# A diffusion transformer block on one core: maxima transposed in one rounded product and sent in three transfers, with halves of the preparation moved between beats

## The chip, the cores and the metric

The kernel runs on one core of a Trainium2 chip. The core has five engines that run their own instruction streams and meet through semaphores: TensorE (PE in the profile, with its weight loads as PEld), VectorE (DVE), ScalarE (ACT), GpSimd (POOL) and SyncE (SP, which here only issues DMA transfers). The metric is the device time of one execution in microseconds (us); the median of three runs is 724.68 us.

## The reference, cut to what matters

The block works on 16 batches of 256 tokens with 256 channels, 16 heads of 16 channels, and a context of 256 tokens for each batch, all in fp32:

```python
x_norm = modulate(_ln(x), shift_a, scale_a)
q, k, v = split(x_norm @ W_qkv + b_qkv)              # self-attention ("source")
x = x + gate_a * (softmax(q k^T * scale) v @ W_proj + b_proj)
q_c = _ln(x) @ W_qc + b_qc                           # cross-attention ("context")
k_c, v_c = split(_ln(context) @ W_kvc + b_kvc)
x = x + softmax(q_c k_c^T * scale) v_c @ W_cproj + b_cproj
x = x + gate_m * (gelu(modulate(_ln(x), shift_m, scale_m) @ W_mlp1 + b_mlp1) @ W_mlp2 + b_mlp2)
```

A softmax needs the maximum of each row of scores, or any number near it: a shift that is the same for a whole row cancels.

## The kernel before, in words

**Split numbers.** Most products are made from two fp32r halves of each fp32 number, a rounded "high" part (`xTh`, `h_q`) and the remainder, "low" (`xTl`, `l_q`). So each prepared operand takes a pass that writes the high half (by ScalarE) and one that writes the low half (by VectorE as value minus high half, or by ScalarE and GpSimd in two steps: ScalarE copies the full value to a tile `y`, GpSimd subtracts).

**Units.** There are 32 attention units: 16 of sources ("s", self-attention of one batch) and 16 of contexts ("c", cross-attention of one batch). The first five are sources; then s and c alternate, and the last five are contexts. While unit n runs its attention, the kernel prepares units n+1 to n+4 and finishes units n-1 to n-3. In the long middle part there are thus two kinds of unit in turn. In this text an **A unit** is one whose running attention is a context's (n is even): it prepares the queries of a context (`q2`, two units on), transposes the normalized source of unit n+3 (`q3`, kind "s"), and normalizes the context tokens of unit n+4 (`lc`). A **B unit** runs a source's attention: it prepares the queries of a source, transposes the context of unit n+3, and normalizes the source of unit n+4 (`ls`).

**Beats.** A unit has eight beats, `beat(n, k)` for k from 0 to 7, and every engine follows its instructions in program order, SP's transfers included. The order of the work is thus the order of the code in `beat`. In each beat

- PE makes four products `s<-big` (scores of the next unit, one pair of heads, into the PSUM tile `s`) and VectorE takes their maxima, `TENSOR_REDUCE mxs<-s`. The tile `s` has one buffer, so PE's next `s` products wait for the reduction;
- PE makes four products `st<-big` (transposed scores of this unit) and ScalarE takes the exponential (`pt<-st`);
- in beats 1, 3, 5 and 7 PE runs two "lanes": 24 half-height products of two preparations side by side (`ps_q`, `ps_k`, `ps_v`, `ps_P`); in beats 0, 2, 4 and 6 it multiplies probabilities with values (`o<-pt,v`). In beat 1 of every unit, and in beat 5 of B units, eight small transpositions (`psT`) are put between the `s` products of this beat and of the next.

**Maxima.** The scores are shifted by a row that is added to the product: row 63 of each half of the queries' tile holds minus the maximum. Maxima stand with queries on partitions, the row needs them along the free dimension. So in beats 2 and 6 PE multiplies `mxs` with an identity (`o<-ident,mxs`, `m_cols`, L767), just ahead of that beat's `o` products; ScalarE negates the result into a tile `m` (`m_send`, L775), and SP sends it into the rows 63, four transfers each time.

**Divisors.** The sums of the softmax of unit n-1 (`S`) come to VectorE by a transfer (`pull_sums`, issued in beat 0), VectorE takes the reciprocal (`recip`), SP writes it to DRAM (`rd<-S`, `spread`) and reads it back spread over all partitions (`R<-rd`, `back`, L1292); GpSimd multiplies (`U<-U,R`) in beat 0 of the next unit.

**Norms.** For a layernorm VectorE makes statistics of the two halves of the tokens (`BATCH_NORM_STATS2`, `st`) and folds them (`mv`); GpSimd makes the reciprocal root (`rs`, two instructions) and normalizes (`xn`, two instructions). The lines of `beat` that the change touches are L1212 to L1300.

Of the kernel before, what the change touches and what calls it, by code (L numbers as in the profile page):

```python
# [21 lines left out]
def pixart_block(  # L22
# [357 lines left out]
    def transposed(src, name, scale=None, pool=False):  # L380
# [61 lines left out]

        o.full, o.rest_pool, o.place = full, rest_pool, place
# [67 lines left out]
    def to_stack(W, src, bias, dst, which, name):  # L511
# [19 lines left out]
        def high():  # L531
            o.hi = work.tile([P, KC, N], F32R, tag="qkh", name=f"h_{name}", bufs=3)
            for f in range(KC):
                ACT.activation(o.hi[:, f], o.ps[:, f * N:(f + 1) * N], AF.Identity, bias=bias[f])
# [190 lines left out]
    def place_of_max(u, g):  # L725

        w, i = (2 + g // 2, g % 2) if u.n == 0 else (2 + u.n % 2, g - 1) if g in (1, 2) else ((u.n - (g == 0)) % 2, g == 0)
        return mxs[w][:, 8 * i:8 * i + 8].rearrange("p (r a t) -> p r a t", r=2, t=NT)  # L730
# [29 lines left out]
    def m_turn(u, hf, pst=None):  # L760

        if pst is None:
            pst = ps_gen(f"psm_{u.n}_{hf}", SHORT)
        PE.transpose(pst[:16, :P], mxs[2 + hf][:, :16], ident)
        return pst

    def m_cols(w, pst):  # L767

        for j in range(2):
            PE.matmul(pst[32 * j:32 * j + 32, :64], w, ident[:, 64 * j:64 * j + 64], start=True, stop=True,
                      tile_position=(0, 32 * j))

    def m_send(pst, *parts):  # L775


        m = work.tile([64, 64], F32R, tag="m2", name="m2", bufs=1)
        ACT.mul(m, pst[:64, :64], -1.0)
        for u, g, row in parts:  # L780
            for j in range(2):
                to = u.q[63:P:64, 2 * g:2 * g + 2].rearrange("r a (t q) -> r a t q", t=NT)[..., 64 * j:64 * j + 64]
                SP.dma_start(to.bitcast(F32), m[32 * j + row:32 * j + row + 8].bitcast(F32))

    def m_row(u, hf, pst):
# [3 lines left out]
        for g in range(2):  # L789
            a = 4 * hf + 2 * g  # L790
            SP.dma_start(u.q[63:P:64, a:a + 2].bitcast(F32), m[8 * g:8 * g + 8].bitcast(F32))
# [369 lines left out]
    def beat(n, k):  # L1161
# [17 lines left out]
        if k == 4 and q2:  # L1179
            q2.Q.high()  # L1180
            q2.Q.send_high()
# [36 lines left out]
        elif k == 1:  # L1218
# [4 lines left out]
            if lc:  # L1223
                lc.ln[0].steps[0]()
# [5 lines left out]
        elif k == 2:  # L1230
            exps()
            if cur:
                parts = [(cur, 3, 0)] * (n > 0) + [(nxt, 0, 8)] * bool(nxt)
# [4 lines left out]
            if ls:  # L1238
                ls.ln[0].steps[0]()
            elif prev:  # L1240
                p1.recip()
                p1.spread()
            if not (q3 and q3.kind == "c"):
                spare(n)
        elif k == 3:
            if q3:
                q3.T[0].high()
            exps()
            if q3 and q3.kind == "c" and n < nu - 4:
                q3.T[0].full()  # L1250
# [7 lines left out]
            if q3 and q3.kind == "s":  # L1258
                q3.T[0].low()
            if prev and ls:  # L1260
                p1.recip()
                p1.spread()
            if lx and n == nu - 4:
                lx.T[0].parts[2]()
        elif k == 4:
# [5 lines left out]
            if q2:  # L1271
                q2.Q.low()
                q2.Q.send_low()
            if q3 and q3.kind == "c":
                if n < nu - 4:
                    q3.T[0].rest_pool()
                spare(n, not lc)
            if ls:
                ls.ln[0].steps[1]()
                ls.ln[0].steps[2]()  # L1280
                ls.ready = True
        elif k == 5:
# [13 lines left out]
        elif k == 6:  # L1296
# [141 lines left out]
```

## Time and profile before

| what | us |
|---|---|
| three runs: lowest, median, highest | 722.59, 724.68, 724.86 |
| the profiled execution: its own time | 722.92 |
| its span, from the first to the last instruction | 721.1 |
| an A unit in the middle, from one first reduction to the next (189.84 to 205.24) | 15.40 |
| the B unit behind it (205.24 to 221.02) | 15.78 |
| PE busy in the A unit and in the B unit | 15.18, 15.60 |
| VectorE busy in the two | 13.67, 13.16 |
| ScalarE busy in the two | 12.66, 13.28 |
| GpSimd busy in the two | 9.54, 12.31 |

The attention units fill the span from about 32 us to 510 us; what follows is the MLP, which the change does not touch. The profiled execution is 1.8 us longer than its span. The granted TensorE clock is 1.00 in all stretches.

### The profile page before, as it was taken

What the parts mean: (1) busy time and instruction counts of PE and PEld (TensorE: products, weight loads), DVE (VectorE), ACT (ScalarE), POOL (GpSimd) and SP (SyncE); (2) the same over time, 40 slices, a digit from 0 to 9 for tenths busy, and PEclk for the clock granted to TensorE, in tenths of its full rate; (3) what the DMA queues carried; (4) which work ended last, traced back from release to release, by engine and by line L of the source; (5) the groups of instructions that cost most, each with busy time, mean ns of one, the idle gap of its engine ahead of it and who ended that gap; (6) DMA issues with size and microseconds to landing.
All of it is one profiled execution on the core that took longest, in us unless ns stands there. A gap on an engine that the chain in (4) does not pass through costs nothing.

```text
span 721.1 us, 23569 instructions
## 1 busy us (share of the span) xinstructions
PE 704.2 (98%) x9359; PEld 600.5 (83%) x9359; DVE 566.5 (79%) x895; ACT 551.0 (76%) x956; POOL 520.5 (72%) x519
## 2 busy tenths in 40 slices
PE   9999999999999999999999999999999999999997
PEld 8777788788877878787778787877779999999997
DVE  5878888988888888778888888888765777777753
ACT  5677888888888888787888888877867677676661
POOL 7665778886776768676686698987766988676552
PEclk9999999999999999999999999999999999999999
DMA  7465455354545536454545556545332223223122
GB/s 238 166 201 200 151 185 194 134 182 167 176 161 186 177 138 189 160 177 150 184 164 193 172 186 204 166 153 206 102 104 87 89 59 89 69 66 86 48 59 74
DMA packets 82921, 106.22 MB, mean 147 GB/s; under 512 B 18970, under 2 KB 45916, under 8 KB 82812
## 3 DMA queue, kind: packets, MB, share of 16 engines
q1 hardware_dynamic: 81916, 104.37, 44.0%
q8 instruction: 74, 1.21, 0.8%
q10 hardware_dynamic: 896, 0.35, 0.2%
q14 instruction: 35, 0.29, 0.1%
HBM read 35.89 MB, written 8.98 MB: 62 GB/s over the span
## 4 chain that ended last, share of the span: by engine, by line
PE 75%; DVE 13%; DMA 4%; issue 2%; POOL 2%; SPq 2%; ACT 1%; POOLq 0%; ACTq 0%; DVEq 0%
PE s L51 18%; PE st L51 13%; PE ph L51 12%; PE o L51 10%; DVE mxs L51 9%; PE ps_kc L51 3%; PE ps_q L51 3%; PE ps_P_s L51 2%; PE ps_k L51 2%; PE ps_v_c L51 2%; SPq L51 2%; PE ps_qc L51 2%; DMA x<-in_x_dram 2%; PE ps_v_s L51 1%; DMA U_s<-oT 1%
## 5 line engine op out<-in xcount | busy, mean ns | idle before, releaser
L51 DVE TENSOR_REDUCE mxs<-s 128x4 f32<-128x1024 f32 x252 | 307.6, 1221 | 65.3 <-PE s L51 60.0
L51 ACT ACTIVATE pt<-st 128x1024 f32<-128x1024 f32 x256 | 262.6, 1026 | 74.6 <-PE st L51 70.4
L51 PE MATMUL s<-big 63*128 63x256 f32 x1008 | 132.9, 322 | 10.9 <-DVE mxs L51 4.3
L51 PE MATMUL o<-pt,v 128*32 128x256 f32 x2048 | 141.6, 384 | 0.0
L51 PEld LDWEIGHTS s<-big 63*128 63x128 f32 x1008 | 82.4, 185 | 70.4 <-DVE mxs L51 62.3
L51 PE MATMUL st<-big 64*128 64x256 f32 (+1 forms) x1040 | 112.4, 285 | 0.3 <-ACT pt L51 0.2
L51 PE MATMUL ph<-xTh_m,wself 128*128 128x256 f32 x512 | 99.6, 280 | 0.0
L51 POOL TENSOR_TENSOR hl<-hf,hh 128x512 fp32r<-128x512 f32 x60 | 80.2, 1354 | 19.2 <-ACT hh L51 19.2
L51 PEld LDWEIGHTS st<-big 64*128 64x128 f32 (+1 forms) x1040 | 85.7, 186 | 3.0 <-ACT pt L51 1.4
L51 PEld LDWEIGHTS o<-pt,v 128*32 128x32 f32 x2048 | 67.0, 109 | 21.7
L51 PEld LDWEIGHTS ph<-xTh_m,wself 128*128 128x128 f32 x512 | 81.9, 188 | 1.2 <-issue 0.4
L51 PE MATMUL ph<-xTl_m,wself 128*128 128x256 f32 x256 | 70.9, 277 | 0.0
L51 ACT ACTIVATE hf<-ph,bT 128x256 f32<-128x256 f32 x112 | 47.0, 473 | 20.6 <-PE ph L51 20.3
L51 ACT ACTIVATE hh<-ph,bT 128x256 fp32r<-128x256 f32 x112 | 47.0, 473 | 19.3 <-PE st L51 8.3
L51 PEld LDWEIGHTS ph<-xTl_m,wself 128*128 128x128 f32 x256 | 48.1, 188 | 0.0
L51 DVE TENSOR_SCALAR xn_m<-x,mv_m,rs_m 128x256 f32<-128x256 f32 x28 | 33.5, 1236 | 15.0 <-POOL rs_m L51 15.0
L51 PE MATMUL s<-big,hh 128*128 128x256 f32 x256 | 45.2, 277 | 0.0
L51 POOL TENSOR_SCALAR rs_c<-mv_c 128x2 f32<-128x2 f32 x16 | 3.6, 228 | 53.5 <-DVE mv_c L51 53.3
L51 POOL TENSOR_SCALAR xn_q<-x,mv_q,rs_q 128x256 f32<-128x256 f32 x32 | 38.9, 1226 | 1.7
L51 POOL TENSOR_SCALAR xn_c<-c,mv_c,rs_c 128x256 f32<-128x256 f32 x32 | 38.9, 1226 | 1.7
L51 PE MATMUL st<-big,hh 128*128 128x256 f32 x224 | 39.5, 276 | 0.0
L51 PEld LDWEIGHTS s<-big,hh 128*128 128x128 f32 x256 | 38.7, 188 | 0.0
(225 smaller groups left out, 2156.9 us busy)
## 6 DMA issues: line engine op xcount, KB each, us to landing
big<-h_k SPq DMA_DIRECT2D x32, 256.0 KB
big<-h_kc SPq DMA_DIRECT2D x32, 256.0 KB
big<-h_qc SPq DMA_DIRECT2D x32, 256.0 KB
big<-h_q SPq DMA_DIRECT2D x30, 256.0 KB
big<-l_k SPq DMA_DIRECT2D x16, 256.0 KB
g<-gd SPq DMA_DIRECT2D x16, 256.0 KB
U_s<-oT SPq DMA_DIRECT2D x32, 128.0 KB
R_s<-rd_s SPq DMA_DIRECT2D x16, 256.0 KB
```

Of the source, the lines that this page charges most:

```text
L51: i = f(*a, **k)
```

## The change

**Maxima.** `mxs` becomes fp32r (rounded), 16 columns for each of four sets in place of 32, and the identity gets an fp32r copy. `m_cols` makes one product of 128 columns in one strip of the array; before it made two fp32 products of 64 columns in two strips. The reductions write their columns so that four neighbouring pairs of heads can go in one transfer: in beat 2 there are two transfers, in beat 6 one, of 512-byte rows; before there were four and four, of 256-byte rows.

**Halves.** Where the unit three on is a source (`apart`: A units, and the first units), the source's high half is made in two pieces before and after the exponential of beat 3, its low half in beats 3 and 4, one piece each; the queries' high half is made in two pieces around the exponential of beat 4, and is sent behind it; the queries' low half moves from beat 4 to beat 5.

**The contexts' remainder.** Where the unit three on is a context, ScalarE's copy `y_c` and GpSimd's subtraction in beat 4 go, and VectorE subtracts from PSUM in beat 3.

**Norms.** The context's statistics are made in beats 1 and 2 (one half each) and the norm is folded and applied in beat 2, before in beat 1 and beat 5. The source's statistics move from beat 2 to beats 5 and 6, folding and applying from beat 4 to beat 6.

**Divisors.** The reciprocal is taken in beat 2 in all units (before: beat 3 in B units); `back` is issued at the start of beat 4, before at the end of beat 5.

```diff
-    mxs = const.tile([P, 4, 32], F32, name="mxs")
-    POOL.memset(mxs, 0.0)
+    mxs = const.tile([P, 4, 16], F32R, name="mxs")
+    POOL.tensor_copy(mxs, wz[:, :64].rearrange("p (a b) -> p a b", a=4))
...
+    identr = const.tile([P, P], F32R, name="identr")
+    POOL.tensor_copy(identr, ident)
...
+        def high_of(f):
+            if f == 0:
+                o.xT = [work.tile([P, KC, N], F32R, tag=f"xT{c}", name=f"xT{c}_{name}", bufs=4) for c in "hl"]
+            ACT.activation(o.xT[0][:, f], o.ps[:, f * N:(f + 1) * N], AF.Identity, scale=scale[f])
+        def low_of(f):
+            DVE.scalar_tensor_tensor(o.xT[1][:, f], o.ps[:, f * N:(f + 1) * N], scale[f],
+                                     o.xT[0][:, f], ALU.mult, ALU.subtract)
...
-        for j in range(2):
-            PE.matmul(pst[32 * j:32 * j + 32, :64], w, ident[:, 64 * j:64 * j + 64], start=True, stop=True,
-                      tile_position=(0, 32 * j))
+        PE.matmul(pst[:16, :P], w, identr, start=True, stop=True, tile_position=(0, 0))
...
-        m = work.tile([64, 64], F32R, tag="m2", name="m2", bufs=1)
-        ACT.mul(m, pst[:64, :64], -1.0)
-        for u, g, row in parts:
-            for j in range(2):
-                to = u.q[63:P:64, 2 * g:2 * g + 2].rearrange("r a (t q) -> r a t q", t=NT)[..., 64 * j:64 * j + 64]
-                SP.dma_start(to.bitcast(F32), m[32 * j + row:32 * j + row + 8].bitcast(F32))
+        m = work.tile([16, P], F32R, tag="m", name="m", bufs=1)
+        ACT.mul(m, pst[:16, :P], -1.0)
+        for u, a, n, row in parts:
+            SP.dma_start(u.q[63:P:64, a:a + n].bitcast(F32), m[row:row + 4 * n].bitcast(F32))
...
-        if k == 4 and q2:
-            q2.Q.high()
-            q2.Q.send_high()
+        apart = q3 and q3.kind == "s"
+        if k == 4:
+            if prev:
+                p1.back()
+            if q2:
+                q2.Q.high((0,) if apart else (0, 1))
+            if q2 and not apart:
+                q2.Q.send_high()
...
             if lc:
-                lc.ln[0].steps[0]()
+                lc.ln[0].stat(0)
...
-            if ls:
-                ls.ln[0].steps[0]()
-            elif prev:
+            if prev:
                 p1.recip()
                 p1.spread()
+            if lc:
+                lc.ln[0].stat(1)
+                lc.ln[0].steps[1](False)
             if not (q3 and q3.kind == "c"):
                 spare(n)
+            if lc:
+                lc.ln[0].pow()
+                lc.ln[0].steps[2]()
+                lc.ready = True
         elif k == 3:
-            if q3:
+            if apart:
+                q3.T[0].high_of(0)
+            elif q3:
                 q3.T[0].high()
             exps()
-            if q3 and q3.kind == "c" and n < nu - 4:
-                q3.T[0].full()
+            if apart:
+                q3.T[0].high_of(1)
...
-            if q3 and q3.kind == "s":
-                q3.T[0].low()
-            if prev and ls:
-                p1.recip()
-                p1.spread()
-            if lx and n == nu - 4:
+            if apart:
+                q3.T[0].low_of(0)
+            if lx:
                 lx.T[0].parts[2]()
...
-            if q2:
+            if apart:
+                q3.T[0].low_of(1)
+                if q2:
+                    q2.Q.high((1,))
+                    q2.Q.send_high()
+            elif q2:
                 q2.Q.low()
                 q2.Q.send_low()
             if q3 and q3.kind == "c":
-                if n < nu - 4:
-                    q3.T[0].rest_pool()
                 spare(n, not lc)
-            if ls:
-                ls.ln[0].steps[1]()
-                ls.ln[0].steps[2]()
-                ls.ready = True
         elif k == 5:
...
-            if lc:
-                lc.ln[0].steps[1]()
-                lc.ln[0].steps[2]()
-                lc.ready = True
-            if prev:
-                p1.back()
+            if apart and q2:
+                q2.Q.low()
+                q2.Q.send_low()
+            if ls:
+                ls.ln[0].stat(0)
...
-                    m_send(cur.po[:, 1], (nxt, 1, 0), (nxt, 2, 8))
+                    m_send(cur.po[:, 1], (nxt, 2, 4, 0))
...
+            if ls:
+                ls.ln[0].stat(1)
+                ls.ln[0].steps[1]()
+                ls.ln[0].steps[2]()
+                ls.ready = True
```

The instructions below stand around beats 0 to 6 of the A unit that starts at 189.84 us in the profile (n = 10). First VectorE before; a reduction opens each beat's share, and the first row shown is that of beat 0:

```order
L51 TENSOR_REDUCE mxs<-s 128x4
L51 SCALAR_TENSOR_TENSOR l_kc_3727<-ps_kc_3573,bP,h_kc_3701 128x256 x2
L51 TENSOR_REDUCE mxs<-s 128x4
L51 BN_STATS st_c_3776<-c_3616 128x6 x2
L51 TENSOR_REDUCE mxs<-s 128x4
L51 RECIPROCAL S_s_3660<-S_s_3660 128x32
L51 TENSOR_REDUCE mxs<-s 128x4
L51 SCALAR_TENSOR_TENSOR xTl_s_3832<-psT_s_3737,sc_107,xTh_s_3831 128x256 x2
L51 TENSOR_REDUCE mxs<-s 128x4
L51 SCALAR_TENSOR_TENSOR l_qc_3888<-ps_qc_3736,bP,h_qc_3864 128x256 x2
L51 TENSOR_REDUCE mxs<-s 128x4
L51 BN_AGGR mv_c_3930<-st_c_3776 128x2 x2
```

and in the change, from beat 1's statistics on:

```order
L51 BN_STATS st_c_3699<-c_3533 128x6
L51 TENSOR_REDUCE mxs<-s 128x2x2
L51 RECIPROCAL S_s_3573<-S_s_3573 128x32
L51 BN_STATS st_c_3699<-c_3533 128x6
L51 BN_AGGR mv_c_3737<-st_c_3699 128x2 x2
L51 TENSOR_REDUCE mxs<-s 128x2x2
L51 SCALAR_TENSOR_TENSOR xTl_s_3761<-psT_s_3660,sc_109,xTh_s_3760 128x256
L51 TENSOR_REDUCE mxs<-s 128x2x2
L51 SCALAR_TENSOR_TENSOR xTl_s_3761<-psT_s_3660,sc_109,xTh_s_3760 128x256
L51 TENSOR_REDUCE mxs<-s 128x2x2
L51 SCALAR_TENSOR_TENSOR l_qc_3857<-ps_qc_3659,bP,h_qc_3794 128x256 x2
L51 TENSOR_REDUCE mxs<-s 128x4 x2
```

Beat 2 now holds the reciprocal, one half of the statistics and the fold; beats 3 and 4 hold one piece of `xTl_s` each; the low half of the queries stands in beat 5.

SP's transfers in the same unit, from the second half of the sums (beat 0) to the maxima of beat 6, before:

```order
L51 DMA S_s_3660<-oT_3612 64x1x32
L51 DMA big_79<-l_kc_3727 32x4x512
L51 DMA U_s_3659<-oT_3612 64x512
L51 DMA big_80<-m_3808 2x4x64 x2
L51 DMA big_82<-m_3808 2x4x64 x2
L51 DMA rd_s_3815<-S_s_3660 128x32
L51 DMA big_79<-h_qc_3864 32x4x512 x2
L51 DMA big_79<-l_qc_3888 32x4x512
L51 DMA R_s_3939<-rd_s_3815 128x1x512
L51 DMA big_82<-m_3965 2x4x64 x4
```

and in the change:

```order
L51 DMA S_s_3573<-oT_3529 64x1x32
L51 DMA big_81<-l_kc_3650 32x4x512
L51 DMA U_s_3572<-oT_3529 64x512
L51 DMA big_82<-m 2x4x128
L51 DMA big_84<-m 2x4x128
L51 DMA rd_s_3734<-S_s_3573 128x32
L51 DMA R_s_3792<-rd_s_3734 128x1x512
L51 DMA big_81<-h_qc_3794 32x4x512 x2
L51 DMA big_81<-l_qc_3857 32x4x512
L51 DMA big_84<-m 2x8x128
```

Three transfers of maxima stand where eight stood, and the read `R_s` is now ahead of the three transfers of queries. PE's order is the same but for the product of maxima.

GpSimd in the B unit in front of it, from beat 1's norm to the products with `R` of the next unit's beat 0, before:

```order
L51 TENSOR_SCALAR xn_q_3449<-x_3_2521,mv_q_3443,rs_q_3446 128x256 x2
L51 TENSOR_TENSOR xTl_c_3500<-y_c_3504,xTh_c_3499 128x512
L51 TENSOR_TENSOR t_c_3293<-t_c_3293,x_0_1411 128x512
L51 TENSOR_SCALAR rs_s_3567<-mv_s_3564 128x2
L51 TENSOR_TENSOR rs_s_3567<-rs_s_3567,mhalf 128x2
L51 TENSOR_SCALAR xn_s_3570<-x_3366,mv_s_3564,rs_s_3567 128x256 x2
L51 TENSOR_TENSOR U_c_3323<-U_c_3323,R_c_3614 128x512
```

and in the change:

```order
L51 TENSOR_SCALAR xn_q_3381<-x_3_2477,mv_q_3375,rs_q_3378 128x256 x2
L51 TENSOR_TENSOR t_c_3229<-t_c_3229,x_0_1391 128x512
L51 TENSOR_SCALAR rs_s_3581<-mv_s_3578 128x2
L51 TENSOR_TENSOR rs_s_3581<-rs_s_3581,mhalf 128x2
L51 TENSOR_SCALAR xn_s_3584<-x_3298,mv_s_3578,rs_s_3581 128x256 x2
L51 TENSOR_TENSOR U_c_3255<-U_c_3255,R_c_3459 128x512
```

The subtraction `xTl_c` is gone; the norm of the source keeps its place in the row, and waits for a fold that VectorE now makes in beat 6 in place of beat 4.

More of the change, by code (lines that the diff above doesn't have):

```diff
@@ L529, in second, with high @@
             high()
-        def high():
-            o.hi = work.tile([P, KC, N], F32R, tag="qkh", name=f"h_{name}", bufs=3)
-            for f in range(KC):
+        def high(fs=range(KC)):
+            if 0 in fs:
+                o.hi = work.tile([P, KC, N], F32R, tag="qkh", name=f"h_{name}", bufs=3)
+            for f in fs:
                 ACT.activation(o.hi[:, f], o.ps[:, f * N:(f + 1) * N], AF.Identity, bias=bias[f])
@@ L725, in place_of_max @@
     def place_of_max(u, g):
[L729 to L730 removed]
+        if u.n == 0 or g in (1, 2):
+            w, i = (2 + g // 2, g % 2) if u.n == 0 else (2 + u.n % 2, g - 1)
+            return mxs[w].rearrange("p (r a t) -> p r a t", r=2, t=NT)[:, :, 2 * i:2 * i + 2]
+        i = int(g == 0)
+        return mxs[(u.n - i) % 2][:, 8 * i:8 * i + 8].rearrange("p (r a t) -> p r a t", r=2, t=NT)
     def s_tile(u, g, par, t, bank=None, home=sp):
@@ L788, in m_row @@
         ACT.mul(m, pst[:16, :P], -1.0)
-        for g in range(2):
-            a = 4 * hf + 2 * g
-            SP.dma_start(u.q[63:P:64, a:a + 2].bitcast(F32), m[8 * g:8 * g + 8].bitcast(F32))
+        SP.dma_start(u.q[63:P:64, 4 * hf:4 * hf + 4, :].bitcast(F32), m.bitcast(F32))
     def t_part(u, pair, par):
```

5 lines of the change are left out of this document (3 added, 2 removed).

## Prediction

> **What bounds the kernel now.** I read the page first, then the timelines of an A unit for VectorE and PE, then SP's queue, then the waits.
>
> ```profile
> PE 704.2 (98%) x9359; PEld 600.5 (83%) x9359; DVE 566.5 (79%) x895; ACT 551.0 (76%) x956; POOL 520.5 (72%) x519
> ```
>
> PE is hardly ever idle and no other engine is above 79%. But a share does not say which wait ends last in a beat. VectorE (start, length, what, idle time ahead and its releaser), beats 2 to 6 of the A unit:
>
> ```profile
> 193.80 1.23 DVE L51 TENSOR_REDUCE mxs<-s 128x4 f32<-128x1024 f32 x1
> 195.50 0.35 DVE L51 RECIPROCAL S_s<-S_s 128x32 f32<-128x32 f32 x1 [0.47 <-DMA S_s<-oT]
> 195.87 1.23 DVE L51 TENSOR_REDUCE mxs<-s 128x4 f32<-128x1024 f32 x1
> 197.01 0.87 DVE L51 SCALAR_TENSOR_TENSOR xTl_s<-psT_s,sc,xTh_s 128x256 fp32r<-128x256 f32 x2
> 197.79 1.22 DVE L51 TENSOR_REDUCE mxs<-s 128x4 f32<-128x1024 f32 x1
> 198.93 0.87 DVE L51 SCALAR_TENSOR_TENSOR l_qc<-ps_qc,bP,h_qc 128x256 fp32r<-128x256 f32 x2
> 199.71 1.21 DVE L51 TENSOR_REDUCE mxs<-s 128x4 f32<-128x1024 f32 x1
> 200.84 0.24 DVE L51 BATCH_NORM_AGGREGATE mv_c<-st_c 128x2 f32<-128x6 f32 x2
> 201.53 1.23 DVE L51 TENSOR_REDUCE mxs<-s 128x4 f32<-128x1024 f32 x1 [0.45 <-PE s L51]
> ```
>
> and PE over the same time, with the `o` block of beat 0 on top:
>
> ```profile
> 189.96 1.07 PE L51 MATMUL o<-pt,v 128*32 128x256 f32 x16
> ...
> 194.22 0.25 PE L51 MATMUL o<-ident,mxs 128*32 128x64 f32 x2
> ...
> 194.36 1.03 PE L51 MATMUL o<-pt,v 128*32 128x256 f32 x14
> 195.32 0.51 PE L51 MATMUL s<-big 63*128 63x256 f32 x4
> ...
> 197.26 0.40 PE L51 MATMUL s<-big 63*128 63x256 f32 x4
> ...
> 199.06 0.50 PE L51 MATMUL s<-big 63*128 63x256 f32 x4
> ```
>
> The reader is to compare the end of each `s` block with the start of the next reduction. Beat 3: 195.32 + 0.51 = 195.83, reduction at 195.87. There PE sets the pace, 0.04 us ahead, and VectorE's wait costs nothing: the reciprocal that waited 0.47 us is over at 195.85. In beat 6 VectorE waits 0.45 us for PE. Beat 4: 197.66, reduction at 197.79, right behind the two `xTl_s` (197.01 and 0.78 for the pair). So VectorE is 0.09 us too late. Beat 5: 199.56 and 199.71, 0.11 us too late behind `l_qc`; but the reduction after it (201.53) waits for PE all the same, so this one is absorbed. And `s` of beat 5 (199.06) follows the end of beat 4's reduction (199.01), not the end of the values' products. Hence in an ordinary unit only PE's own work and those 0.09 us can be won.
>
> The other thing to win lies in units with longer beats. The first two groups below are from the unit at 252 us (VectorE, then SP), the third is from the beat 2 of the B unit behind it, the last from the table of waits (total us, times, longest):
>
> ```profile
> 256.16 1.22 DVE L51 TENSOR_REDUCE mxs<-s 128x4 f32<-128x1024 f32 x1
> 258.90 0.35 DVE L51 RECIPROCAL S_s<-S_s 128x32 f32<-128x32 f32 x1 [1.52 <-DMA S_s<-oT]
> 259.17 1.16 DVE L51 TENSOR_REDUCE mxs<-s 128x4 f32<-128x1024 f32 x1
> ```
>
> ```profile
> 257.04 0.60 SPq L51 DMA_DIRECT2D S_s<-oT  x1
> ```
>
> ```profile
> 274.22 0.75 DVE L51 BATCH_NORM_STATS2 st_s<-x 128x6 f32<-128x256 f32 x2 [0.57 <-DMA x<-in_x_dram]
> 274.89 1.20 DVE L51 TENSOR_REDUCE mxs<-s 128x4 f32<-128x1024 f32 x1
> ```
>
> ```profile
> DVE S_s L51 <- DMA S_s<-oT: 8.0, 10, 2.0
> ...
> DVE st_s L51 <- DMA x<-in_x_dram: 3.6, 5, 1.6
> ```
>
> Here beat 2 takes 259.17 - 256.16 = 3.01 us in place of 2.07 (193.80 to 195.87): VectorE's queue stands behind a reciprocal whose sums SP issued only at 257.04.
>
> **The change, part by part.** *The product of maxima (PE).* With it an `o` block lasts 194.22 to 195.39, 1.17 us; without, 1.07. So the two fp32 products cost 0.10. What one fp32r product of 128 columns costs no row shows. The nearest fp32r row is this, of the start, a chain of 12 products of 256 columns:
>
> ```profile
> 10.17 1.39 PE ps_k L51 x12
> ```
>
> 0.116 each, so 0.058 for half the columns: 0.042 won. At the pace of the fp32 pair now there (0.10 for 64 columns) 128 columns in one strip take 0.20: 0.10 lost. I take the fp32r pace, because its row has the same number type; the other end is kept. There are 63 such products (two in 31 units, one in the last). Beat 6 of the 11 middle B units may keep nothing (below), leaves 52: -2.2 us; ends -2.6 and +6.3.
>
> *Halves.* Beats 3 and 4 of an A unit each get one piece of 0.39 (half of 0.78) behind the reduction, ending 0.6 us ahead of PE; the 0.09 us of beat 4 goes in 11 units (n = 2 to 22, each second one): -1.0. The low half of the queries moves into beat 5: 1.14 from the reduction's start to the next instruction (195.87 to 197.01) + 0.78 = 1.92, where PE takes 1.82 (199.71 to 201.53). The 0.10 is absorbed too: the reduction of beat 6 ends at 201.53 + 1.23 = 202.76, and the `s` block that waits for it stands behind `o`, which ends at 202.81 and with two first products of lanes still between:
>
> ```profile
> 201.78 1.03 PE L51 MATMUL o<-pt,v 128*32 128x256 f32 x14
> ```
>
> In units 0 and 1 one half of the sources' statistics comes into the same beat 5: + 0.33 (half of 274.22 to 274.89), so 2.25 against 1.82, 0.43 more; I count +0.25 for each after such slack, +0.5.
>
> *Reciprocals and statistics.* SP in the A unit, ahead of, in and behind beat 2:
>
> ```profile
> 193.62 0.59 SPq L51 DMA_DIRECT2D S_s<-oT  x1
> ...
> 195.76 2.29 SPq L51 DMA_DIRECT2D big<-m  x4
> 198.16 0.33 SPq L51 DMA_DIRECT2D rd_s<-S_s  x1
> ...
> 199.85 0.55 SPq L51 DMA_DIRECT2D big<-l_qc  x1
> 200.59 0.68 SPq L51 DMA_DIRECT2D R_s<-rd_s  x1
> 203.23 2.22 SPq L51 DMA_DIRECT2D big<-m  x4
> ...
> 215.92 0.68 SPq L51 DMA_DIRECT2D R_c<-rd_c  x1
> ```
>
> Four maxima transfers hold SP 2.2 us, one a quarter of it: three fewer in beat 6 bring the sums of the next unit's beat 0 forward by up to 1.65 us, here from 193.62 to about 192, as ScalarE allows. That takes away the long waits: of the 8.0 us, seven ordinary ones are 3.3 and cost nothing; of the other 4.7 the three beats lose 0.94 for each 1.52 waited, 3.0 us in all. The source's statistics, now three beats later, no longer wait for `x`: of 3.6 us one wait of 1.6 is in the prologue; the other 2.0, at the same 0.94 in 1.52, are -1.2. Together -4.2. The new load of beat 2, reciprocal 0.27 (258.90 to 259.17), statistics 0.33, fold 0.24 behind 1.14, is 1.98 against PE's 2.03 (193.80 to 195.83), so nothing if the sums are there by 194.94. The context's remainder, 0.68 on VectorE in beat 3, (an estimate: the pair `xTl_s` does the same work in 0.87) stands in the place of a reciprocal: 1.14 + 0.68 = 1.82, as long as PE's own beat with lanes. GpSimd and ScalarE lose a pass each per B unit: in the rows above nothing waits for either in beats 3 and 4, zero.
>
> *The norm of the source, two beats later.* GpSimd now, the reduction of beat 6, and PE's first transposition of the norm:
>
> ```profile
> 215.73 0.23 POOL L51 TENSOR_SCALAR rs_s<-mv_s 128x2 f32<-128x2 f32 x1
> ...
> 216.86 2.44 POOL L51 TENSOR_SCALAR xn_s<-x,mv_s,rs_s 128x256 f32<-128x256 f32 x2
> 220.65 1.29 POOL L51 TENSOR_TENSOR U_c<-U_c,R_c 128x512 f32<-128x512 f32 x1 [1.36 <-DMA big<-l_q]
> ```
>
> ```profile
> 217.09 1.23 DVE L51 TENSOR_REDUCE mxs<-s 128x4 f32<-128x1024 f32 x1 [0.60 <-PE s L51]
> ```
>
> ```profile
> 222.53 0.22 PE L51 MATMUL psT_s<-ident,xn_s 64*128 64x64 f32 x1
> ```
>
> The fold will end at 217.09 + 1.14 + 0.33 + 0.24 = 218.80; GpSimd takes 215.73 to 219.30, 3.57 us, so 222.37 and two handoffs. PE asks at 222.53. The cover is just used up: zero, but what beat 6's product wins is lost again (why 52, above). `U_c` then moves from 220.65 to about 222.5; three passes of 1.3 us at most end by 226.4, and PE needs them in beat 3, which reduces at 195.87 + 31.18 (both units of the table) = 227.05.
>
> *Transfers moved.* `R` goes ahead of the queries on SP, and waits there for `rd` to land; `l_qc` is issued at about 201.7 (VectorE ends it at 199.71 + 1.14 + 0.87 - 0.09) in place of 199.85, and PE's `s` of the next unit needs it at 204.80 (0.44 ahead of the reduction of 205.24 in the table). Landing times of others:
>
> ```profile
> 258.32 2.72 DMA U_s<-oT
> ...
> 269.97 4.23 DMA x<-in_x_dram
> ```
>
> At 2.72 it lands at 204.4, in time; at 4.23 at 205.9, 1.1 too late. `U_s` runs from SBUF to SBUF as `l_qc` does, so I take zero for most units, and 1.0 us for a late one: +1.0; ends 0 and 11 x 1.1 = 12.
>
> **Sum.** -2.2 - 1.0 + 0.5 - 4.2 + 1.0 = -5.9 us on the profiled execution's 722.92 (span 721.1 and 1.8 around it): 717.0. The median of the runs, 724.68, is 1.8 above that execution, so against it this is 7.7 us or 1.1%.
>
> **Rivals.** *The product is no faster for being rounded.* Then +6.3 replaces -2.2: 725.5, no change. For it: no row has an fp32r product under 256 columns. Against it: only the fp32r row above. The Trainium skill, "TensorE: Matmul & The Clock Gate", Part 3, The mechanism, says that products in different strips of the array overlap, and the change gives the second strip up; at equal pace that rule gives this rival's time. The trace bears the rule out, two products of 64 columns costing 0.10.
>
> *The queries land too late (slower).* If `l_qc` takes over 3.1 us from issue to landing in A units, PE's `s` stalls in beat 0, 1.1 us at 4.23: 11 units, 717.0 - 1.0 + 12 = 728. For it: `R` now stands ahead, and `U_c` at 220.65 began 4.7 us after the issue of its `R` (215.92). Against it: `R` is issued three us ahead of `l_qc`. The Trainium skill, "DMA: Bandwidth & Descriptors", Two DMAs through the same engine are not ordered, has descriptors of one queue start in order on each engine, so the queries would wait behind `R`; with `R` issued about when `rd` is today, 198.5, by 4.7 and 0.6 for each of three transfers `l_qc` would land at 205.0, 0.2 late, and the sum would be 717.0 - 1.0 + 2.2 = 718.2. No row here shows that order.
>
> *The waits come back elsewhere.* If the sums come no sooner than now, reciprocal, statistics and fold start at 195.50 and end at 196.33, 0.46 later than today's reduction; I count 0.3 of it past the slack of beat 3, in 11 units: 717.0 + 3.3, and without the -3.0 it is 723. This is also the case in which the change does not do what it says.
>
> **How the numbers follow.** My forecast gets 0.56, its own range 713 to 720. The equal product gets 0.17 (722 to 727), the late queries 0.13 (723 to 735), the waits elsewhere 0.14 (719 to 724). 0.3% is about what a measurement of this kernel can tell from no change: 722.5 to 726.9. Faster: 0.56 + 0.02 + 0.09 = 0.67; the same: 0.12 + 0.03 + 0.05 = 0.20; slower: 0.03 + 0.10 = 0.13. The range 712 to 727 reaches from all good ends (-2.6 - 1.0 - 4.2, no late transfer, and some 3 for waits that I have not priced) to the equal product's end.
>
> **What would show it.** In the profile after: `o` blocks with maxima of about 1.13 us (1.27 for the first rival); reductions of beat 4 0.04 behind `s`; no long waits for `S` or `x`; PE's `s` in beat 0 with no wait for `l_q` or `l_qc` (the second rival shows there, a beat 0 over 2.5 us); no wait of PE for `xn_s` in beat 1. The prediction is wrong if beat 1 of A units gets longer, or if an `s` block begins to wait for a transfer.

## The result, and the profile after

The changed kernel takes 754.06 us (median of 4 runs, 749.37 to 760.19), the kernel before 723.91 us on the same chip: a ratio of 1.042, with a 95% interval of 1.035 to 1.050. It is slower, where 717.0 us was forecast. The profiled execution took 753.57 us, with a span of 751.8.

Busy times, and the shares of the chain that ended last, on the page of the kernel after:

```profile
PE 713.3 (95%) x9170; PEld 592.8 (79%) x9170; DVE 579.0 (77%) x910; ACT 552.7 (74%) x941; POOL 503.1 (67%) x505
...
PE 72%; DVE 9%; DMA 9%; issue 4%; ACT 3%; SPq 2%; POOL 0%; ACTq 0%; DVEq 0%; POOLq 0%
```

PE was at 98% before. Its busy time grew by 9.1 us (704.2 to 713.3) while the span grew by 30.7 us: most of the loss is waiting, and the chain says for whom, a transfer (DMA, 9%). The waits (total us, times, longest):

```profile
PE s L51 <- DMA big<-l_qc: 9.5, 6, 2.9
...
DVE xTl_s L51 <- ACT xTh_s L51: 6.9, 13, 0.7
...
PE s L51 <- DMA U_c<-oT: 5.6, 2, 2.8
...
PE s L51 <- DMA big<-l_q: 3.5, 4, 1.5
...
DVE st_s L51 <- DMA x<-in_x_dram: 1.7, 1, 1.7
...
DVE S_c L51 <- DMA S_c<-oT: 0.7, 1, 0.7
```

The last two rows are the cured waits. Those for sums of sources were 8.0 us before and are gone, those for sums of contexts were

```profile
DVE S_c L51 <- DMA S_c<-oT: 3.7, 3, 2.0
```

before and are a single one of 0.7 now; statistics waited 3.6 us for `x` before, and now only once, in the prologue. The first four rows came with the change (before, `l_q` and `xTh_s` had one such wait each, 0.5 and 0.6 us). The row with `U_c<-oT` belongs to the queries too: by the records of issue and landing in the trace, PE starts in both of its cases 0.14 and 0.35 us behind the landing of `l_qc`, and ahead of that of `U_c`. So it is in all 13 waits of PE's `s` for a transfer: PE starts 0.13 to 0.35 us behind the landing of `l_q` or `l_qc`.

Mean length of each beat, from one start of `TENSOR_REDUCE mxs<-s` to the next, worked out from VectorE's timeline (A units 4 to 22, B units 5 to 21, contexts 23 to 28):

| | 0 | 1 | 2 | 3 | 4 | 5 | 6 | 7 | unit |
|---|---|---|---|---|---|---|---|---|---|
| before, A | 2.13 | 1.83 | 2.40 | 1.90 | 1.91 | 1.82 | 1.89 | 1.86 | 15.74 |
| after, A | 2.13 | 1.83 | 2.14 | 2.14 | 1.82 | 1.92 | 1.90 | 3.07 | 16.95 |
| before, B | 2.13 | 1.83 | 2.16 | 1.85 | 2.13 | 1.83 | 2.07 | 1.87 | 15.86 |
| after, B | 2.28 | 1.83 | 2.14 | 1.88 | 2.13 | 1.83 | 2.14 | 2.24 | 16.46 |
| before, 23 to 28 | 2.13 | 1.96 | 1.94 | 1.86 | 2.13 | 1.83 | 2.07 | 2.05 | 15.97 |
| after, 23 to 28 | 2.13 | 1.86 | 2.10 | 1.87 | 2.13 | 1.83 | 2.20 | 3.06 | 17.19 |

Beat 7 ends when PE has made the first `s` of the next unit. A unit in which that goes badly, the A unit from 296.96 to 315.26: SP's queue first, then PE, then the piece of the chain that ended last.

```profile
302.99 1.20 SPq L51 DMA_DIRECT2D big<-m  x2
304.29 0.33 SPq L51 DMA_DIRECT2D rd_s<-S_s  x1
307.66 0.63 SPq L51 DMA_DIRECT2D R_s<-rd_s  x1
308.38 1.23 SPq L51 DMA_DIRECT2D big<-h_qc  x2
309.70 0.55 SPq L51 DMA_DIRECT2D big<-l_qc  x1
310.66 0.57 SPq L51 DMA_DIRECT2D big<-m  x1
```

```profile
301.34 0.23 PE L51 MATMUL o<-identr,mxs 128*16 128x128 f32 x1
301.51 1.07 PE L51 MATMUL o<-pt,v 128*32 128x256 f32 x16
302.51 0.51 PE L51 MATMUL s<-big 63*128 63x256 f32 x4
...
306.45 0.50 PE L51 MATMUL s<-big 63*128 63x256 f32 x4 [0.37 <-DVE mxs L51]
...
314.71 0.51 PE L51 MATMUL s<-big 63*128 63x256 f32 x4 [2.38 <-DMA big<-l_qc]
```

```profile
309.01 0.70 DVE mxs L51
309.70 4.88 DMA big<-l_qc
314.58 0.14 issue
314.71 0.51 PE s L51 x4
```

SP stands still from 304.62 to 307.66, until `rd` has landed; the queries behind `R` are issued late, and `l_qc` then takes 4.88 us to land. This is one of the two A units in which `rd` is late (the last section says why): in the others `l_qc` is issued 0.7 us sooner in the unit. Of the records of issue and landing in the trace, this unit's (us from issue to landing, time of landing; the right column is the A unit of before at 189.84):

```
            after                   before
rd_s        3.32 -> 307.61          2.37 -> 200.53
R_s         4.44 -> 312.10          3.55 -> 204.13 (issued last)
h_qc        4.22 -> 312.61          2.60 -> 201.14
h_qc        4.23 -> 313.25          2.65 -> 201.80
l_qc        4.88 -> 314.58          2.57 -> 202.42
```

Behind `R` the three transfers of queries land one after the other, 0.5, 1.1 and 2.5 us after it, though each takes 2.6 us in the unit of before, where `R` is issued last.

A wait of PE has a second price. The granted clock of the profiled execution is 0.995, where it was 1.000 before. In two stretches of 3.4 us it is half; the first begins 0.5 us behind the end of the wait shown:

```profile
315.20:318.60 3.40, 3.40 (x33) 1.90 (x32) 2.01 (x3) 1.61 (x2) 0.33 (x1) 0.50 0.39 140
```

The figure ahead of the last two is the granted clock of this stretch. Beat 0 of the B unit that begins there takes 3.50 us, that of the other eight 2.13: all of the 0.15 us in the table's beat 0 is this one beat. Two such stretches make some 2.7 of the 30.7 us (an estimate: twice 1.37, though the second begins while PE still waits).

### The profile page after: what moved, and what is told of

Read it like the earlier page. It is cut to its first block, busy times and chain, and to the rows that moved or that the text cites. A ratio compares the mean times of both kernels' runs of the same rounds, so it can differ in the third digit from the quotient of the medians.

```text
span 751.8 us, 22952 instructions
## 1 busy us (share of the span) xinstructions
PE 713.3 (95%) x9170; PEld 592.8 (79%) x9170; DVE 579.0 (77%) x910; ACT 552.7 (74%) x941; POOL 503.1 (67%) x505
## 4 chain that ended last, share of the span: by engine, by line
PE 72%; DVE 9%; DMA 9%; issue 4%; ACT 3%; SPq 2%; POOL 0%; ACTq 0%; DVEq 0%; POOLq 0%
PE s L51 18%; PE st L51 13%; PE ph L51 12%; PE o L51 11%; DVE mxs L51 7%; DMA big<-l_qc 4%; PE ps_q L51 3%; DMA big<-l_q 3%; PE ps_kc L51 3%; PE ps_P_s L51 2%; SPq L51 2%; PE ps_qc L51 2%; PE ps_v_c L51 2%; PE ps_k L51 1%; ACT xTh_s L51 1%
## 5 line engine op out<-in xcount | busy, mean ns | idle before, releaser
L51 DVE TENSOR_REDUCE mxs<-s 128x4 fp32r<-128x1024 f32 x252 | 308.2, 1223 | 87.9 <-PE s L51 79.1
L51 PE MATMUL o<-pt,v 128*32 128x256 f32 x2048 | 138.8, 389 | 0.0
L51 PEld LDWEIGHTS st<-big 64*128 64x128 f32 (+1 forms) x1040 | 87.5, 187 | 3.0 <-ACT pt L51 1.3
L51 PEld LDWEIGHTS o<-pt,v 128*32 128x32 f32 x2048 | 53.8, 110 | 35.9 <-issue 1.4
L51 POOL TENSOR_SCALAR rs_s<-mv_s 128x2 f32<-128x2 f32 x16 | 3.7, 228 | 55.3 <-DVE mv_s L51 55.0
L51 ACT COPY oT<-o 128x512 f32<-128x512 f32 x64 | 37.4, 584 | 3.0 <-PE o L51 3.0
```

Of the source, the lines that this page charges most:

```text
L51: i = f(*a, **k)
```

## The experiments

Each kernel was timed beside the kernel before on its own chip (723.29, 724.93 and 724.56 us in the three groups), so it is the ratios that are compared.

**Which part costs the time.** Theory: `R` ahead of the queries. Rival: the halves, which make ScalarE and VectorE send the queries' parts later. Two kernels undo one of them each.

In e1 `R` is back behind the queries:

```diff
         if k == 4:
-            if prev:
-                p1.back()
...
         elif k == 5:
...
+            if prev:
+                p1.back()
```

> The changed kernel with one part undone: the read of the divisors (R) is issued at the end of beat 5 again, behind the three transfers of queries. Theory 1 (the queries land late because R stands ahead of them in SP's queue): the long beats 7 and 0 go, some 22 to 27 us, and the time is 727 (724 to 731); what is left over the kernel before is the product of maxima (63 x 0.07 us) and the halves (11 x 0.20 us). Theory 2 (they land late because the low half of the queries is made and sent a beat later): about 745, since that part stays. Both at work: between, 732 to 740.

In e2 the halves of sources and queries are as before (their low parts too):

```diff
-                q2.Q.high((0,) if apart else (0, 1))
-            if q2 and not apart:
-                q2.Q.send_high()
+                q2.Q.high()
+                q2.Q.send_high()
...
-            if apart:
-                q3.T[0].high_of(0)
-            elif q3:
+            if q3:
                 q3.T[0].high()
             exps()
-            if apart:
-                q3.T[0].high_of(1)
```

> The changed kernel with another part undone: halves of sources and queries in whole passes as before (queries' low half in beat 4 and sent there), R still ahead of the queries. Theory 1: the units with contexts alone and the B units keep their long beats, A units get shorter since the low half is issued 1.9 us sooner: about 740 (735 to 746). Theory 2: the long beats of A units go and with them most of the loss: 727 to 732.

Measured: e1 729.13 us, ratio 1.008 (1.005 to 1.011); e2 745.25 us, 1.030 (1.026 to 1.034). `R` ahead is the main cost. Then `R` ahead alone, as an edit of the kernel before (e3, the diff), and both undone in the kernel after (e4, the edits of e1 and e2 together):

```diff
+        if k == 4 and prev:
+            p1.back()
         if k == 4 and q2:
             q2.Q.high()
...
-            if prev:
-                p1.back()
             v = unit(n + 5)
```

> The kernel before with one part of the change alone: R is issued at the start of beat 4, ahead of the queries. Theory 1: beats 7 and 0 get long as in the changed kernel, 735 to 750. Theory 2: no change, 723 to 725.

> The changed kernel with R behind the queries and the halves undone; what is left of the change is the product and the transfers of maxima, the contexts' remainder on VectorE, the norms' places and the sooner reciprocal. Both theories: no long beats, 63 x 0.07 = 4.4 us lost by the product, some 4 us won by the waits for sums and for x that are gone: 723 to 726. If it is above 732, a third part makes the queries late.

e3 took 786.48 us, 1.088 (1.083 to 1.093): in the kernel before, the one moved transfer costs more than twice what it does in the changed one, and my 735 to 750 was far too low. e4 took 722.17 us, 0.998 (0.996 to 1.000). So the cost of `R` ahead is 23 us without the halves (e2 less e4), 25 with them; that of the halves is 7.0 us with `R` behind (e1 less e4). The chain of e3 shows the same transfer:

```profile
219.97 4.88 DMA big<-l_qc
```

**Two ways in which R ahead makes the queries late.** `R` has to wait for `rd` to land, and SP with it (theory W); and its packets stand ahead of the queries' in the queue (theory Q). e5 keeps the queue and takes the wait away, by reading data that landed long ago (it leaves out the division, for its `R` holds zeros); e6 keeps the wait and leaves `R` behind.

Both are edits of e4. e5:

```diff
+    rdc = dram.tile([2, 4, 2 * N], F32, name="rdc", bufs=1)
+    SP.dma_start(rdc, wz[:, :32])
...
-            SP.dma_start(o.R, o.rd.rearrange("g h n -> (g h) n").unsqueeze(1).to_broadcast([8, HD, 2 * N]))
+            SP.dma_start(o.R, rdc.rearrange("g h n -> (g h) n").unsqueeze(1).to_broadcast([8, HD, 2 * N]))
...
         if k == 4:
+            if prev:
+                p1.back()
...
-            if prev:
-                p1.back()
```

> The kernel with both changes undone (R behind the queries, halves as before; 722.17 us) with R issued ahead of the queries again, but read from DRAM data that was written in the prologue, so that SP does not wait for rd to land. The division by the sums is left out by this (R holds zeros), and every instruction and transfer stays. Theory Q (the queries are late because their packets stand behind R's in the queue): they stay late, 738 to 748 us. Theory W (they are late because SP stands still until rd has landed, some 1.1 to 3 us, and R and the queries all start later): 722 to 727 us, and no wait of PE for the queries.

e6:

```diff
+        def touch():
+            t = work.tile([1, 32], F32, tag="tch", name=f"tch_{name}", bufs=1)
+            SP.dma_start(t, o.rd[0, 0:1, 0:32])
...
         if k == 4:
+            if prev:
+                p1.touch()
```

> The same kernel (722.17 us), R behind the queries, with one added transfer of 128 bytes out of rd ahead of the queries, which makes SP wait for rd to land but brings no R ahead of the queries. Theory W alone: SP's wait is enough, 735 to 748 us. Theory Q alone: nothing stands ahead in the queue, 722 to 725 us. If both are needed together: 722 to 728 us here, and under 728 us in the run with the old data too.

Measured: e5 733.08 us, 1.012 (1.008 to 1.016), between the two theories; e6 726.6 us, 1.002 (0.9995 to 1.004). The two alone make 1.4% and 0.4% over e4's 0.998; together, in e2, they make 3.2%. They add up against one slack: against e4 the queries land 1.0 us later in e6, 2.0 in e5 and 3.1 in e2. Medians over the units between 100 and 390 us, from the records of issue and landing (the largest in brackets), all in us after the issue of `rd`:

| | `rd` lands | `R` issued | `R` lands | `l_q`/`l_qc` issued | `l_q`/`l_qc` lands |
|---|---|---|---|---|---|
| before | 1.41 | 2.36 | 6.57 | 1.70 | 4.55 (6.59) |
| e4, R behind | 1.42 | 3.33 | 7.44 | 2.69 | 5.09 (7.72) |
| e6, wait alone | 1.42 | 4.03 | 8.14 | 3.37 | 6.12 (8.40) |
| e5, queue alone | 1.42 | 0.42 | 4.94 | 2.71 | 7.05 (8.10) |
| e2, both | 1.42 | 1.48 | 6.14 | 3.52 | 8.17 (10.33) |
| after, both and halves | 1.42 | 1.48 | 6.10 | 4.73 | 8.24 (10.81) |
| e1, halves, R behind | 1.41 | 4.35 | 8.86 | 3.72 | 7.11 (8.89) |
| e3, before and R ahead | 1.47 | 1.53 | 6.26 | 4.01 | 8.19 (9.80) |

When does PE ask? In the A unit of e4 whose first reduction starts at 315.65, SP's queue has

```profile
322.98 0.33 SPq L51 DMA_DIRECT2D rd_s<-S_s  x1
```

that is 7.33 us into the unit. An A unit of e4 that nothing disturbs lasts 15.55 us, and its last `s` starts 0.55 ahead of the next unit's reduction (204.81 and 205.36 in the unit at 189.84): 15.55 - 0.55 - 7.33 = 7.7 us after `rd`. In a B unit it is 8.1. With the eight maxima transfers of before it is 204.80 - 198.16 = 6.6 in an A unit. Against these the last column explains the order of the times: one cause alone (6.1, 7.1) stays under 7.7, both (8.2) do not, and in e3 the same 8.2 meets 6.6, some 1.6 us late in nearly every unit. The table lumps the two kinds of unit. By kinds, the queries of the changed kernel land a median of 8.6 us after `rd` in A units and 8.1 in B units, so the A units lose more. e6 loses its 0.4% mostly in beat 2 of some A units (mean 2.31 us, e4 2.14), not in beat 7 (1.91, e4 1.85). In the middle units e5 indeed loses next to nothing (A 15.61 and B 15.93 us, e4 15.57 and 15.92); its 11 us come behind unit 23, where a weight transfer of the MLP stands in the same queue. One unit there, SP's queue and PE:

```profile
438.06 0.43 SPq L51 DMA_DIRECT2D w<-in_L_xcond_W_mlp_dram  x1
438.58 0.64 SPq L51 DMA_DIRECT2D R_c<-rdc  x1
439.27 1.24 SPq L51 DMA_DIRECT2D big<-h_qc  x2
440.62 0.55 SPq L51 DMA_DIRECT2D big<-l_qc  x1
```

```profile
447.27 0.51 PE L51 MATMUL s<-big 63*128 63x256 f32 x4 [1.29 <-DMA S_s<-oT]
```

By the records of landing `R_c` lands there at 445.18, 6.60 us after its issue, the queries at 445.58, 446.24 and 446.92, and PE starts at 447.27. The row names `S_s<-oT`; it lands at 449.00 and so can't have released PE. The records of landing settle which transfer it was, the bracket doesn't.

**The halves.** The new wait `xTl_s <- ACT xTh_s` is VectorE's first low piece. In the unit above:

```profile
303.06 1.22 DVE L51 TENSOR_REDUCE mxs<-s 128x4 fp32r<-128x1024 f32 x1
304.79 0.48 DVE L51 SCALAR_TENSOR_TENSOR xTl_s<-psT_s,sc,xTh_s 128x256 fp32r<-128x256 f32 x1 [0.51 <-ACT xTh_s L51]
305.19 1.21 DVE L51 TENSOR_REDUCE mxs<-s 128x4 fp32r<-128x1024 f32 x1
```

```profile
302.87 0.46 ACT L51 ACTIVATE xTh_s<-psT_s,sc 128x256 fp32r<-128x256 f32 x1
303.30 1.03 ACT L51 ACTIVATE pt<-st 128x1024 f32<-128x1024 f32 x1
304.22 0.47 ACT L51 ACTIVATE xTh_s<-psT_s,sc 128x256 fp32r<-128x256 f32 x1
```

The first low piece needs only the first high piece, which ends at 303.33. It starts when the second has ended, at 304.69: the wait is for the tile, and the second piece stands behind the exponential. e9, an edit of e1, puts that piece ahead of the exponential again:

```diff
             if apart:
                 q3.T[0].high_of(0)
+                q3.T[0].high_of(1)
...
             exps()
-            if apart:
-                q3.T[0].high_of(1)
```

> The kernel with R behind the queries and the halves as changed (729.13 us), with both pieces of the source's high half made ahead of the exponential again; all else stays halved (low pieces in beats 3 and 4, queries' low half in beat 5). Theory P (VectorE's first low piece waits for the tile, that is for ScalarE's second piece behind the exponential, and this costs 0.2 us in beat 3 of each A unit): beat 3 of A units back from 2.13 to 1.92 us, beat 4 stays at 1.82, 726 to 727 us. Rival (beat 3 is longer for another reason, such as the exponential that now comes sooner): beat 3 stays at 2.1, 729 us.

VectorE in beat 3 of e9:

```profile
264.33 1.23 DVE L51 TENSOR_REDUCE mxs<-s 128x4 fp32r<-128x1024 f32 x1
265.47 0.48 DVE L51 SCALAR_TENSOR_TENSOR xTl_s<-psT_s,sc,xTh_s 128x256 fp32r<-128x256 f32 x1
266.18 1.23 DVE L51 TENSOR_REDUCE mxs<-s 128x4 fp32r<-128x1024 f32 x1 [0.23 <-PE s L51]
```

The wait is gone; beat 3 of A units is 1.87 us (e1 2.13), beat 4 stays at 1.83. That is theory P. The time, 728.18 us, ratio 1.005 (1.003 to 1.007) against 1.008 (1.005 to 1.011) for e1, moved as it should by the ratios (0.3%, 2.3 us), though not as far down as the 726 to 727 us that I had written; the two intervals overlap, so it is the beats that show the cause, not the time. What is left over e4 are beat 5 (1.92 against 1.82) and late queries in beat 7 (2.09 against 1.85): the low half comes a beat later, and of the 7.7 us its landing takes a median of 7.1.

**The product and the transfers of the maxima**, on e4. e7 puts both back as they were before the change, e10 only the product in two strips, e11 makes the one product fp32, and e8 makes it 256 columns wide.

e10 (e7 has these lines too, with the old places of the maxima and so eight transfers):

```diff
-        PE.matmul(pst[:16, :P], w, identr, start=True, stop=True, tile_position=(0, 0))
+        for j in range(2):
+            PE.matmul(pst[32 * j:32 * j + 32, :64], w, identr[:, 64 * j:64 * j + 64], start=True, stop=True,
+                      tile_position=(0, 32 * j))
...
+            for j in range(2):
+                to = u.q[63:P:64, a:a + n].rearrange("r a (t q) -> r a t q", t=NT)[..., 64 * j:64 * j + 64]
+                SP.dma_start(to.bitcast(F32), m[32 * j + row:32 * j + row + 4 * n].bitcast(F32))
```

e10 and e11 (`mxs` is F32 in both):

```diff
-    identr = const.tile([P, P], F32R, name="identr")
-    POOL.tensor_copy(identr, ident)
+    identr = ident
```

e8:

```diff
-        PE.matmul(pst[:16, :P], w, identr, start=True, stop=True, tile_position=(0, 0))
+        PE.matmul(pst[:16, :2 * P].rearrange("p (a b) -> p a b", a=2), w, identr.unsqueeze(1).to_broadcast([P, 2, P]), start=True, stop=True, tile_position=(0, 0))
```

> The kernel with R behind and halves as before (722.17 us), with the maxima as before the change too: fp32 products in two strips, eight transfers a unit. If the rounded product is the slower one, as o blocks of 1.24 us against 1.17 say, 62 products give back 0.07 us each: 717 to 719 us. If the fewer transfers are what cured the waits for S, these come back, some 3 us: 720 to 722 us.

> The kernel with R behind and halves as before (722.17 us), with the rounded product of the maxima made 256 columns wide (the identity twice) in place of 128; nothing reads the added columns. If a rounded product is slow only because it is narrow, 256 columns take 0.12 us as in the chains of the lanes, less than the 0.17 of 128 now: o blocks of about 1.19 us, 718 to 720 us. If the cost grows with the columns, 0.34 us: o blocks of about 1.41 us, 731 to 734 us.

> The kernel with R behind and halves as before (722.17 us), with the product of the maxima as two fp32 products of 64 columns in two strips, as before the change, but with the change's order of the columns, so that six transfers do in place of eight (four in beat 2, two in beat 6). If the strips are what made the old product cheap, o blocks of 1.17 us, 62 times 0.07: 718 us. If one more transfer in beat 6 and two in beat 2 bring the waits for S back: 722 us or more (eight transfers gave 736).

> The kernel with R behind and halves as before (722.17 us), with the one product of 128 columns in fp32 in place of rounded; the three transfers stay. If rounding makes the product no cheaper, the o blocks stay at 1.24 us: 721 to 723 us. If it takes the 0.20 us of the pace of the fp32 pair before, o blocks of 1.27 us: 723 to 725 us. If an fp32 product passes the columns four times (0.23 us against 0.06 for one pass), o blocks of 1.3 us or more: 726 us or more.

PE at the head of an `o` block with maxima, in this order: e8, e10, e11.

```profile
291.63 0.29 PE L51 MATMUL o<-identr,mxs 128*16 128x256 f32 x1
291.85 1.07 PE L51 MATMUL o<-pt,v 128*32 128x256 f32 x16
```

```profile
288.06 0.25 PE L51 MATMUL o<-ident,mxs 128*32 128x64 f32 x2
288.09 0.41 PE L51 MATMUL o<-pt,v 128*32 128x256 f32 x2
288.14 0.23 PE L51 MATMUL o<-ident,mxs 128*32 128x64 f32 x2
288.20 1.03 PE L51 MATMUL o<-pt,v 128*32 128x256 f32 x14
```

```profile
291.23 0.28 PE L51 MATMUL o<-ident,mxs 128*16 128x128 f32 x1
291.25 0.42 PE L51 MATMUL o<-pt,v 128*32 128x256 f32 x3
291.35 0.27 PE L51 MATMUL o<-ident,mxs 128*16 128x128 f32 x1
291.46 1.03 PE L51 MATMUL o<-pt,v 128*32 128x256 f32 x13
```

From the first start to the last end, the median of the 63 blocks of each run, less the 1.07 us of the 65 `o` blocks without maxima (the rows, each rounded, give 0.01 more here and there):

| product | `o` block | cost | kernel, us | ratio to before |
|---|---|---|---|---|
| rounded, 128 columns, one strip (e4) | 1.23 | 0.16 | 722.17 | 0.998 (0.996 to 1.000) |
| rounded, 256 columns, one strip (e8) | 1.29 | 0.22 | 725.04 | 1.002 (0.9995 to 1.003) |
| fp32, 128 columns, one strip (e11) | 1.26 | 0.18 | 723.88 | 0.998 (0.997 to 1.000) |
| fp32, 64 columns in each of two strips (e10) | 1.17 | 0.10 | 720.84 | 0.995 (0.994 to 0.997) |
| the same, eight transfers (e7) | 1.17 | 0.10 | 736.39 | 1.015 (1.010 to 1.021) |

Rounding wins 0.02 us, the second strip was worth 0.09 (1.255 less 1.169). e8 fits neither of its expectations: the second 128 columns cost 0.06, the pace of the prediction's chain (0.058), so a rounded product here has a part of about 0.1 that does not grow with its columns (an estimate from these two widths). e10 is the fastest kernel of the study, 0.5% faster than before, if by less than I expected of it (718). e7 falsified both of its expectations: with the reciprocal in beat 2 of all units, eight transfers are not a few us worse than six but 14 to 16. Its waits for sums are 15.5 and 11.3 us, where e10 has 2.9 and 0.9. They, and one of them (SP's row, then VectorE's):

```profile
DVE S_c L51 <- DMA S_c<-oT: 15.5, 13, 2.7
...
DVE S_s L51 <- DMA S_s<-oT: 11.3, 14, 2.3
```

```profile
294.07 0.59 SPq L51 DMA_DIRECT2D S_s<-oT  x1
```

```profile
296.05 0.35 DVE L51 RECIPROCAL S_s<-S_s 128x32 f32<-128x32 f32 x1 [2.31 <-DMA S_s<-oT]
```

## Why the prediction was wrong

By ratios the runs form a ladder: before to e10 -0.5%, e10 to e4 +0.3%, e4 to e1 +1.0%, e1 to after +3.4%; in us of 724 that is -3.5, +2.0, +7.4 and +24.8, together 30.7. The intervals of e10 and e4 overlap, so the +0.3% is the least sure step. Point by point:

- **"Transfers moved", +1.0 us: this is the step that failed.** It measured 23 to 25 us. The landing of `l_qc` was wrong: 2.72 us after its issue, taken from `U_s<-oT`, a transfer with nothing long ahead of it. Behind `R` it takes a median of 3.8 us in the A units of the profile after, and 3.0 to 5.2, where the prediction left it 3.1; with `R` behind (e1) it takes 2.4. The issue was nearly right: said for 201.7, that is 11.9 us into the unit, it stands at 12.1, and at 12.1 in e1 as well. So SP's wait for `rd` holds up `l_qc` itself only in the two A units with a late `rd` (12.7 and 12.9) and in B units (11.0 in place of 10.0, and then 4.6 us to landing); everywhere it holds up `R`, and so the landing of what stands behind. And the sum counted 11 A units alone, one of them late: the B units lose 0.6 us each and the units from 23 on 1.2.
- **The rival of late queries** (chance 0.13, 728 us) named the mechanism and the place, and was too small, since it too counted 11 A units. The rule that it cited, the Trainium skill, "DMA: Bandwidth & Descriptors", Two DMAs through the same engine are not ordered, says that descriptors of one queue start in order on each engine; the trace agrees, for in the four kernels with `R` ahead (after, e2, e3, e5) the queries land 0.3 to 4.0 us behind `R` and never ahead of it, in e5 too, where nothing else ties them to it. The estimate by that rule, 0.2 us late, was 0.7 short, and came that near in part by luck: it let `R` go at 198.5 without a wait for `rd`, and `R` does go at 198.7 (8.9 us into the unit), because `rd` is issued 1.0 us sooner behind two maxima transfers than behind four. `R` then takes 4.5 us (4.7 said), and `l_qc` lands 2.5 behind it (1.8 said): 205.7, 0.9 late. All these are medians of the ten A units; in the mean their beat 7 is 1.2 us longer, which the last section takes up.
- **Product, -2.2 us:** the cost is 0.16 us, not 0.058. My other end, 0.20 (+6.3 us), was the nearer: against two strips it is 63 times 0.06, some +4. e10 to e4 shows 2.0 of it, since the two strips' transfers bring some waits for `S` back (B units' beat 2 is 2.20 us in e10, 2.14 in e4). The first rival, that rounding makes it no faster, was thus right in its mechanism. The rule beside it, the Trainium skill, "TensorE: Matmul & The Clock Gate", Part 3, The mechanism, that products in different strips overlap, is borne out: 0.10 in two strips against 0.18 in one.
- **Halves, -1.0 us:** beat 4 of A units fell by 0.09 us exactly as said. But beat 3 grew by 0.21 (the wait for the tile, 0.2 of it shown by e9), beat 5 by 0.10, which I had called absorbed, and beat 7 by 0.31 through later queries: +7 us in all. Beat 5 of units 0 and 1 grew from 1.80 to 2.26 us each, as the working said (0.43), where the sum counted 0.25. The wait for the tile could have been read from the code, one tile written in two pieces; I looked at VectorE's load alone.
- **Waits for S and x, -4.2 us:** right. Beat 2 of A units fell from 2.40 to 2.14, the long waits are gone, and the parts that bring this make -3.5 us alone (e10, the transfers six in place of three). The sum had left out the 3.7 us of waits for sums of contexts, which went as well. What I did not see is how much hangs on the transfers: with eight of them the kernel with the sooner reciprocal is 11 us slower than before instead (e7).
- **The norm of the source, 0:** right, PE's `psT_s` does not wait for `xn_s`.
- **The waits elsewhere** (720 to 723 us) did not happen in the changed kernel; e7 shows them, and they cost some 15 us (e7 less e10) where I had put 6.3 on them.

## What to carry to other kernels

A transfer that is moved ahead on a queue has two prices: the time for which the queue's engine stands waiting for its source, and the time for which all transfers behind it land late. Work out both for the last transfer behind it, add them, and set the sum against the slack of the one that needs it: each alone may be hidden (0.4% and 1.4% here, and little in the middle units) while both are not (3.2%), and the same move cost 23 us where the slack was 7.7 and 63 where it was 6.6. Count every kind of unit in which the transfer moves, not only the one that was looked at. Before a pass is cut into pieces, see whether its reader waits for a piece or for the whole tile.

## What the runs showed of the hardware that I had not expected

- A broadcast read of 256 KB (`R`) lands 3.5 to 5.8 us after its issue (medians of the runs 4.0 to 4.6), and the last transfer of queries, which takes 2.4 to 2.7 us in the median ahead of it, takes 4.3 to 4.5 behind it. With a weight transfer just ahead of it in the queue, `R` takes 5.8 to 7.1 us (four units of e5).
- A rounded product of 16 output rows delays the products behind it by 0.16 us at 128 columns and 0.22 at 256, and all 16 `o` products start behind it; of those behind the fp32 product in one strip, the first three start 0.02 us after it (e11). Why the rounded one does not let them was not tried.
- `rd`, 1.4 us as a rule, took 3.3 us in the unit shown. The DMA packets of the stretch from 305 to 307 us have one that is none of the kernel's transfers, an instruction load:

```profile
q8 instruction: 1, 0.02, 3.7%
```

It holds 16 KB and runs from 305.41 to 306.58; the last eight of `rd`'s packets start at 306.56, and 15 of its 16 signs of landing had come by 305.70. It is the same everywhere: in all 13 profiles, each of the 38 `rd` of the first 520 us that took over 2.0 us has an instruction load between 0.7 us behind its issue and 0.3 us ahead of its landing, and none of the 281 that took up to 1.5 us has. Two of the ten A units of the profile after have such an `rd` (3.3 and 3.5 us), and they make 5.7 of the 12.1 us that beat 7 loses in the ten.
- The granted clock fell to half for 3.4 us (once 6.8) during a long wait of PE (1.9 to 4.8 us) or within 1.6 us of its end, after some of these waits and not after others: twice in the profile after, six times in that of e3, whose mean is 0.984. So the times of the kernels with long waits hold some us of lower clock too.
